# Cross-attention, layer 1: one set of token-wise exponentials, turned in 32x32 blocks by VectorE, in place of a second, key-wise set

## Chip, cores and metric

One core of one Trainium2 chip runs the kernel. The metric is the device time of one run in microseconds (us), as the median of several runs. Engines are named PE (TensorE, matrix multiplication; PEld is its weight loads), DVE (VectorE), ACT (ScalarE), POOL (GpSimd) and SP (SyncE, which issues most DMAs). All arithmetic is FP32.

## The reference, cut to what matters

Two cross-attention layers follow each other over the same 128 context rows per batch (B = 2, S = 2048 tokens, width 512).

```
def layer0(q, ctx, mask):              # 16 heads of 64
    qh, kh, vh = heads(q@Wq+bq), heads(ctx@Wk+bk), heads(ctx@Wv+bv)
    attn = einsum('bhqd,bhkd->bhqk', qh, kh) * mask
    attn = exp(attn - max(attn)) * mask
    attn = attn / (sum(attn, -1) + 1e-15)
    x = heads_joined(attn @ vh) @ Wo + bo + q
    return layernorm(x) * gamma + beta

def layer1(query, ctx):                # 16 heads of 32
    q, k, v = heads(query@Wq.T), heads(ctx@Wk.T), heads(ctx@Wv.T)
    logits = (1/sqrt(32)) * einsum('bhqd,bhkd->bhqk', q, k)
    attn = softmax(logits, -1)         # over 128 keys
    ctx1 = heads_joined(attn @ v)
    x = query + ctx1 @ Wo.T + bo
    return layernorm(x) * gamma + beta

out = layer1(layer0(x, ctx, mask), ctx)
```

## The kernel before

The 2 x 2048 tokens are cut into 8 blocks t of 512 tokens; a block has 4 sub-tiles i of 128 tokens. The 16 heads form 4 groups g of 4 heads r. The attention of layer 0 runs first, for all blocks, up to about 390 us. Then stages t = -1 to 7 follow. In stage t three blocks are worked on side by side: the softmax of layer 1 for block t, the output projection and the layer norm of layer 0 and then the queries of layer 1 for the blocks after it (n = t + 1, f = t + 2), and the output projection and layer norm of layer 1 for the block before it (l = t - 1).

The order is written by hand. `steps(t)` returns a list of steps, each a letter with its block and part, and `go` issues them one after the other; every engine executes its own instructions in the order in which they were issued, and waits where one needs a result of another engine. So a step's place in the list is its place in all queues at once, those of the DMAs on SP too.

The letters that matter here:

- X, `maxima(t, g)`: token-wise scores. 16 matmuls (L873) with 32 rows of weights (the queries of 128 tokens) and 128 columns (the keys) on four row tiles of the array put scores of 128 tokens x (4 heads, 4 sub-tiles, 128 keys) into the two PSUM tiles `sc0` and `sc1`. DVE takes the maximum over the keys for heads 2 and 3 (L879) and scales it (`less`, L886), ACT takes eight exponentials (L889); DVE does the maximum for heads 0 and 1 (L893) and subtracts it (L894), ACT takes one exponential of 1024 elements (L897). The result `e` has its tokens on the partitions.
- U, `sums1(t, g)`: DVE adds up each head's 128 exponentials (2048 elements a partition, L903). G, `shares1(t)`: the reciprocals of all sums (L911), into `tops`, beside the maxima.
- M, `turn_maxima(t)`: PE transposes `tops` (L916), DVE copies it out (L918), and SP's queue writes the rows to DRAM and reads them back spread over partitions: per group 1 MB of maxima (`p1`) and 256 KB of shares (`r1`).
- S, `scores1(t, g)`: the same scores a second time, with the keys on the partitions: four matmuls (L948) of 512 columns into `sc0` and `sc1`; DVE subtracts the spread maxima (L967). P1, `exponentials1`: one ACT exponential of 2048 elements (L972).
- V, `attend1(t, g)`: four matmuls (L996) with a head's values (128 keys x 32) as weights and its 512 token columns of exponentials as data, one for each column tile of the array. VD, `scale1`: DVE multiplies the result by the spread shares (L1009).
- E, `project1` (L1026), Y, `rest1` (adds the residual, L1033), I, `moments1`, O, `norm1`, W, `store` (the output DMA): projection and layer norm of block l.
- Pr (`project0`, L671), J, K0, Z, N, R, L: the output projection of layer 0 and its layer norm. T/TW and Q, or TS/PQ/AQ (L822 to L852), turn the result and make the queries.

The last stage, t = 7, has no projections of later blocks. There no maxima are spread: X only takes maxima, and S subtracts them by four more matmuls with a constant matrix `sel` (L955); ACT takes the exponentials from PSUM; the sums come from matmuls with `ones` (L987); and C, `divide1`, takes the reciprocals of 512 columns on DVE (L1015) and multiplies (L1016). After stage 7 come, for block 7, the first halves of four projections, then the second halves, each with its residual, moments and norm.

The two lines that tie the step's place to the queues, and the buffers that S, X and (after the change) V share:

```
    def sc_tiles(name, shape):
        return [p_sc.tile([P, *shape], F32, tag=f"sc{n}", name=f"{name}_{n}") for n in range(2)]
    ...
    for t in range(-1, NB):
        go(steps(t))
```

The pool `p_sc` has one buffer for each tag, so a new user of the score tiles waits until the one before has been read. The values of layer 1 for both batches, `v1`, are made before the stages (L582, copied by ACT in L586) and stay in SBUF.

Of the kernel before, what the change touches and what calls it, by code (L numbers as in the profile page):

```python
# [16 lines left out]
P = 128  # L17
# [7 lines left out]
def two_cross_attentions(  # L25
# [81 lines left out]
    sel = const.tile([P, NG, K], F32, tag="sel", name="sel")  # L107
    for g in range(NG):
        for r in range(4):
            rows = slice(32 * r, 32 * (r + 1))  # L110
            nc.vector.tensor_scalar(
                sel[rows, g, :], ident[rows, 32 * r + g : 32 * r + g + 1].to_broadcast([32, K]),
                -1.0, None, ALU.mult,
            )
# [5 lines left out]
    v1 = const.tile([P, B, D], F32, tag="v1", name="v1")  # L120
# [27 lines left out]
    rows_dram = [dram.tile([2 * NG, 4, TB], F32, tag=f"rows_{t}", name=f"rows_{t}") for t in range(NB)]  # L148
# [57 lines left out]
    with tc.tile_pool(name="w1", bufs=1) as w1, tc.tile_pool(name="a2", bufs=2) as a2, tc.tile_pool(  # L206
# [372 lines left out]
        def values1(b):  # L579
# [6 lines left out]
            nc.scalar.copy(v1[:, b, :], ps)  # L586
# [279 lines left out]
    def maxima(t, g):  # L866
# [10 lines left out]
        to = tops.rearrange("p i (r n) -> p r i n", n=32)[:, :, :, g : g + 1]  # L877
        to = to.rearrange("p r i o -> p r (i o)")
        nc.vector.tensor_reduce(to[:, 2:], ps[1], AX.X, ALU.max)  # L879
        if t == NB - 1:  # L880
            nc.vector.tensor_reduce(to[:, :2], ps[0], AX.X, ALU.max)
            return

        e = fours.tile([P, 4, NQ, K], F32, tag="p1", name=f"e_{t}_{g}")
        less = three.tile([P, 2, NQ], F32, tag="less", name=f"less_{t}_{g}")
        nc.vector.tensor_scalar_mul(less, to[:, 2:, :], -scaling)  # L886
        for r in range(2, 4):
            for i in range(NQ):
                nc.scalar.activation(  # L889
                    e[:, r, i, :], ps[1][:, r - 2, i, :], AF.Exp, bias=less[:, r - 2, i : i + 1],  # L890
                    scale=scaling,
                )
        nc.vector.tensor_reduce(to[:, :2], ps[0], AX.X, ALU.max)  # L893
        nc.vector.tensor_tensor(  # L894
            e[:, :2], ps[0], to[:, :2, :].unsqueeze(3).to_broadcast([P, 2, NQ, K]), ALU.subtract
        )
        nc.scalar.activation(e[:, :2], e[:, :2], AF.Exp, scale=scaling)  # L897
        open_x[t, g] = e

    def sums1(t, g):  # L900

        to = sums.rearrange("p i r n -> p r i n")[:, :, :, g : g + 1]
        nc.vector.tensor_reduce(  # L903
            to.rearrange("p r i o -> p r (i o)"), open_x.pop((t, g)), AX.X, ALU.add
        )

    tTs, probs1, open_x = {}, {}, {}

    def shares1(t):
        share = tops.rearrange("p i (r n) -> p i r n", n=32)[:, :, :, NG : 2 * NG]  # L910
        nc.vector.reciprocal(share, sums)  # L911

    def turn_maxima(t):
# [5 lines left out]
        tTs[t] = tT  # L919
        if t == NB - 1:  # L920
# [307 lines left out]
```

## Time and profile before

| what | value |
|---|---|
| median of 3 runs | 981.69 us (980.66 to 983.73) |
| span of the profiled execution, first to last instruction | 977.3 us |
| profiled execution's own time | not listed apart from its span; the span lies 4.4 us under the median |
| mean granted PE clock | 0.997 |
| busy: PE, DVE, ACT, POOL | 958.0, 731.8, 414.9, 483.3 us |
| steady stages, start to start of X(t,0) | 643.27, 713.14, 783.03, 852.90: 69.9 us each |
| X(7,0), start of the last stage | 916.10 us |

A line of a timeline gives the start and the length of a run of like instructions, the engine, the line of the code, the operation, out<-in with the shapes, how many there were, and in brackets how long the engine was idle before and on whom it waited. Matmuls are listed by passes: an FP32 matmul is two.

### The profile page before, as it was taken

The page shows a single profiled execution, that of the slowest core. Times are in us where ns is not written, and L with a number is a line of the kernel's source. Part 1 is how long each engine was busy: PE and PEld are TensorE (multiplying, and loading weights), DVE is VectorE, ACT ScalarE, POOL GpSimd, SP SyncE. Part 2 cuts the span into 40 slices and gives each one's busy share as a digit, 9 for nine tenths or more (in the row PEclk, how much of TensorE's full clock was granted, in tenths as well). Part 3 has the DMA queues.
Part 4 walks back from the last instruction along what each step waited for, and adds up shares of the span by engine and source line. Part 5 has one row for each costly group of instructions (what it writes and reads, how often), then busy time and mean ns, then how long its engine had stood idle before and what let it go on. Part 6 is the DMA issues. An engine that isn't in the chain of part 4 may idle for free.

```text
span 977.3 us, 12755 instructions
## 1 busy us (share of the span) xinstructions
PE 958.0 (98%) x4628; PEld 448.4 (46%) x4628; DVE 731.8 (75%) x1093; ACT 414.9 (42%) x637; POOL 483.3 (49%) x403
## 2 busy tenths in 40 slices
PE   8999999999999999999999999999999999999996
PEld 4444333333333334474544644645545545545442
DVE  2577777878878872249469869879789689698867
ACT  1145345545534644044534434434344444344351
POOL 1044454543453546685453934925835736546153
PEclk9999999999999999999999999999999999999998
DMA  9314265225223436534632542632723724403311
GB/s 337 126 49 141 55 175 155 56 57 182 60 79 86 120 104 201 181 128 157 243 128 87 188 160 87 238 110 89 263 82 119 251 90 155 167 1 151 111 44 43
DMA packets 51325, 128.46 MB, mean 131 GB/s; under 512 B 9440, under 2 KB 13280, under 8 KB 47680
## 3 DMA queue, kind: packets, MB, share of 16 engines
q1 hardware_dynamic: 49536, 125.03, 38.5%
q0 software_dynamic: 1152, 2.10, 0.9%
q8 instruction: 36, 0.59, 0.3%
q10 hardware_dynamic: 576, 0.53, 0.2%
q14 instruction: 25, 0.20, 0.1%
HBM read 101.46 MB, written 26.18 MB: 131 GB/s over the span
## 4 chain that ended last, share of the span: by engine, by line
PE 76%; DVE 4%; POOL 2%; issue 1%; ACT 0%; POOLq 0%; DVEq 0%; ACTq 0%
PE pso L671 22%; PE ps L347 12%; PE pso L1026 10%; PE psq L822 8%; PE psu L491 5%; PE st L396 4%; PE s L948 3%; PE mx L873 3%; PE u L996 3%; PE psq L860 1%; PE tr L727 1%; PE den L470 1%; PE den L484 1%; DVE sums L903 1%; PE psk L591 1%
## 5 line engine op out<-in xcount | busy, mean ns | idle before, releaser
L435 POOL TENSOR_TENSOR sm<-sm,mask 128x1024 f32<-128x1024 f32 x64 | 150.4, 2372 | 202.4 <-ACT sm L434 191.4
L671 PE MATMUL pso<-wo,uT 128*128 128x512 f32 x512 | 229.2, 599 | 0.2 <-POOL uT L182 0.2
L671 PEld LDWEIGHTS pso<-wo,uT 128*128 128x128 f32 x512 | 94.5, 190 | 117.2 <-issue 109.1
L658 POOL TENSOR_TENSOR rstd<-rstd,mhalf 128x1 f32<-128x1 f32 x64 | 35.2, 550 | 213.8 <-DVE shift L662 213.7
L434 ACT ACTIVATE sm<-sm,ncs 128x1024 f32<-128x1024 f32 x64 | 70.0, 1141 | 107.6 <-DVE ncs L431 107.5
L1026 PE MATMUL pso<-wq,ctx 128*128 128x512 f32 x256 | 115.5, 600 | 0.0
L889 ACT ACTIVATE e<-mx,less 128x128 f32<-128x128 f32 x224 | 60.9, 383 | 83.6 <-DVE less L886 83.6
L972 ACT ACTIVATE p<-p 128x2048 f32<-128x2048 f32 x28 | 53.5, 1911 | 97.2 <-DVE p L967 79.5
L409 DVE CUSTOM_DVE_ANT_1 sm<-st,mask 128x1024 f32<-128x1024 f32 x64 | 75.6, 1217 | 20.9 <-DMA mask<-in_maskT_dram 13.5
L967 DVE TENSOR_TENSOR p<-s,p 128x1024 f32<-128x1024 f32 x56 | 65.8, 1217 | 29.2 <-PE s L948 28.6
L347 PE MATMUL ps<-xt,wq 128*128 128x512 f32 x180 | 83.4, 599 | 0.0
L359 DVE TENSOR_TENSOR q<-ps,q 128x512 f32<-128x512 f32 x75 | 51.9, 692 | 39.5 <-PE ps L347 35.3
L182 POOL TENSOR_TENSOR uT<-uT,r 128x1024 f32<-128x1024 f32 x32 | 75.3, 2362 | 3.7 <-issue 1.7
L1026 PEld LDWEIGHTS pso<-wq,ctx 128*128 128x128 f32 x256 | 46.5, 190 | 57.4 <-issue 48.6
L462 DVE TENSOR_TENSOR fold<-fold,sm 64x2048 f32<-64x2048 f32 x22 | 64.5, 2930 | 2.6 <-ACT fold L456 1.9
L903 DVE TENSOR_REDUCE sums<-e 128x16 f32<-128x2048 f32 x28 | 63.8, 2278 | 1.1 <-ACT e L897 1.1
L396 PE MATMUL st<-q,k 64*128 64x512 f32 x256 | 63.6, 615 | 0.0
L491 PE MATMUL psu<-sm,v 128*32 128x512 f32 x512 | 62.1, 598 | 0.8 <-ACT dens L441 0.7
L347 PE MATMUL ps<-t,s 128*128 128x512 f32 x120 | 56.4, 592 | 0.0
L347 PEld LDWEIGHTS ps<-xt,wq 128*128 128x128 f32 x180 | 33.2, 190 | 46.5 <-issue 46.4
L686 ACT ACTIVATE z<-z,shift,rstd 128x512 f32<-128x512 f32 x32 | 26.0, 814 | 66.9 <-POOL shift L663 66.9
L688 POOL TENSOR_TENSOR y<-z,g 128x512 f32<-128x512 f32 x32 | 40.6, 1269 | 23.1 <-ACT z L686 23.1
(154 smaller groups left out, 1511.0 us busy)
## 6 DMA issues: line engine op xcount, KB each, us to landing
p<-rows SPq DMA_DIRECT2D x28, 1024.0 KB
u<-u SPq DMA_DIRECT2D x32, 512.0 KB
uT<-u SPq DMA_DIRECT2D x32, 512.0 KB
xt<-in_xT_dram SPq DMA_DIRECT2D x16, 512.0 KB
z<-in_x_dram SPq DMA_DIRECT2D x32, 256.0 KB
r<-r SPq DMA_DIRECT2D x32, 256.0 KB
out_dram<-y SPq DMA_DIRECT2D x32, 256.0 KB
r<-rows SPq DMA_DIRECT2D x28, 256.0 KB
```

The source lines that it names most:

```text
L182: nc.gpsimd.tensor_tensor(u, u, r.unsqueeze(1).to_broadcast([P, 2, TB]), ALU.mult)
L347: nc.tensor.matmul(ps, w[:, c, :], x[c] if isinstance(x, tuple) else x[:, c, :], start=(c == 0), stop=(c == 1),)
L396: nc.tensor.matmul(st[n][:, j, :], k0[rows, 2 * g + n, b * K : (b + 1) * K], q[rows, :], start=True, stop=True,)
L409: nc.vector.tensor_tensor_reduce(out=sm, in0=st[n], in1=masks[t].unsqueeze(1).to_broadcast([P, 2, TB]), scale=1.0, scalar=-3.4028234e38, o ...
L434: nc.scalar.activation(s, s, AF.Exp, bias=ncs[:, i + n : i + n + 1])
L435: nc.gpsimd.tensor_tensor(s, s, masks[t].unsqueeze(1).to_broadcast([P, 2, TB]), ALU.mult)
L491: nc.tensor.matmul(ps[32 * j : 32 * (j + 1), :], v0[:, b, d : d + 32], p[j], start=True, stop=True,)
L671: nc.tensor.matmul(ps, uTs[t, n // 2][:, n % 2, i * P : (i + 1) * P], wo0s[n // 2][:, n % 2, :], start=(n == 0), stop=(n == NE - 1),)
L822: nc.tensor.matmul(ps[:, m, :], w[:, c, m * P : (m + 1) * P], y[:, c, :], start=(c == 0), stop=(c == 1),)
L903: nc.vector.tensor_reduce(to.rearrange("p r i o -> p r (i o)"), open_x.pop((t, g)), AX.X, ALU.add)
L967: nc.vector.tensor_tensor(p1[:, at], ps[n], p1[:, at], ALU.subtract)
L1026: nc.tensor.matmul(ps, ctxs[t][g][:, i * P : (i + 1) * P], wo1s[:, g, :], start=(g == 0), stop=(g == NG - 1),)
```

## The change

After the change, X, for all eight blocks, keeps its maxima to itself (`top`), and ACT adds up the eight exponentials of heads 2 and 3 while it makes them (`accum_out`); U adds up only heads 0 and 1. Then DVE transposes `e` in place, in 32x32 blocks (`blocks1`). After that each block of 32 tokens and 32 keys has the keys on its 32 partitions. So V multiplies 32 x 32 blocks: for each quarter k of the keys, each 32-partition row tile a (32 tokens of every sub-tile) and each head r (a column tile) a matmul with 32x32 weights and 128 columns, 64 in all on 16 array tiles, summed over k in the score tiles. For this the values must have each quarter of the keys on each 32 partitions: `v1` goes through DRAM into `v1r`, four copies. `scale1` puts the columns back into order in two instructions. S, P1, C, `sel`, the matmuls with `ones` and the spreading of the maxima go; M turns the shares alone.

In the last stage U also takes the reciprocals of its group's 16 sums, and multiplies `e` by them, on POOL for groups 0 and 1 and on DVE for 2 and 3, ahead of the transposition, which for groups 0 and 1 is a step of its own, UT. V's result is there only copied, one half by DVE and one by ACT. The lists of steps change as shown; V(0,3) moves from the start of stage 1 to the end of stage 0. The scratch for DMA descriptors made by software is set to 2048 bytes.

```diff
-    sel = const.tile([P, NG, K], F32, tag="sel", name="sel")
...
-    v1 = const.tile([P, B, D], F32, tag="v1", name="v1")
...
+    v1_dram = dram.tile([B, K, D], F32, tag="v1", name="v1")
+    rows_dram = [dram.tile([NG, 4, TB], F32, tag=f"rows_{t}", name=f"rows_{t}") for t in range(NB)]
...
-            nc.scalar.copy(v1[:, b, :], ps)
+            v = eight.tile([P, D], F32, tag="z", name=f"v1_{b}")
+            nc.scalar.copy(v, ps)
+            nc.sync.dma_start(v1_dram[b], v)
...
+        top = three.tile([P, 2, 2, NQ], F32, tag="top", name=f"top1_{t}_{g}")
+        less = three.tile([P, 2, NQ], F32, tag="less", name=f"less_{t}_{g}")
         e = fours.tile([P, 4, NQ, K], F32, tag="p1", name=f"e_{t}_{g}")
+        nc.vector.tensor_reduce(top[:, 1], ps[1], AX.X, ALU.max)
+        nc.vector.tensor_scalar_mul(less, top[:, 1], -scaling)
         for r in range(2, 4):
             for i in range(NQ):
                 nc.scalar.activation(
                     e[:, r, i, :], ps[1][:, r - 2, i, :], AF.Exp, bias=less[:, r - 2, i : i + 1],
-                    scale=scaling,
-                )
+                    scale=scaling, accum_out=sums[:, i, r, g : g + 1],
+                )
+        nc.vector.tensor_reduce(top[:, 0], ps[0], AX.X, ALU.max)
         nc.vector.tensor_tensor(
+            e[:, :2], ps[0], top[:, 0].unsqueeze(3).to_broadcast([P, 2, NQ, K]), ALU.subtract
         )
         nc.scalar.activation(e[:, :2], e[:, :2], AF.Exp, scale=scaling)
+        probs1[t, g] = e
 
     def sums1(t, g):
 
+        e = probs1[t, g]
+        to = sums.rearrange("p i r n -> p r i n")[:, :2, :, g : g + 1]
+        nc.vector.tensor_reduce(to.rearrange("p r i o -> p r (i o)"), e[:, :2], AX.X, ALU.add)
+        if t == NB - 1:
+            share = three.tile([P, NQ, 4], F32, tag="share", name=f"share_{t}_{g}")
+            nc.vector.reciprocal(share, sums[:, :, :, g])
+            engine = nc.gpsimd if g < 2 else nc.vector
+            engine.tensor_tensor(
+                e, e, share.rearrange("p i r -> p r i").unsqueeze(3).to_broadcast([P, 4, NQ, K]),
+                ALU.mult,
+            )
+        if t < NB - 1 or g > 1:
+            blocks1(t, g)
+
+    def blocks1(t, g):
+        flat = probs1[t, g].rearrange("p r i k -> p (r i k)")
+        nc.vector.transpose(flat, flat)
...
+    def turn_shares(t):
...
         for r in range(4):
-            nc.sync.dma_start(rows_dram[t][:, r, :], tT[32 * r : 32 * r + 2 * NG, :])
+            nc.sync.dma_start(rows_dram[t][:, r, :], tT[32 * r : 32 * r + NG, :])
         for g in range(NG):
...
+            r = three.tile([P, TB], F32, tag="r1", bufs=4, name=f"r1_{t}_{g}")
+            nc.sync.dma_start(r, rows_dram[t][g].unsqueeze(1).to_broadcast([4, 32, TB]))
+            dens1[t, g] = r
...
     def attend1(t, g, apart=False):
...
+        ps = sc_tiles(f"u1_{t}_{g}", [2, TB])
+        for k in range(4):
+            for a in range(4):
+                of = slice(32 * a, 32 * (a + 1))
+                for r in range(4):
+                    h = 4 * g + r
+                    nc.tensor.matmul(
+                        ps[a // 2][32 * r : 32 * (r + 1), a % 2, :P].rearrange("p (i q) -> p i q", q=32),
+                        v1r[of, b, k, h * HD : (h + 1) * HD], e[of, r, :, k, :],
+                        start=(k == 0), stop=(k == 3),
+                    )
         open_u[t, g] = ps
...
+    def by_rows(x):
+        return x.rearrange("p (i a q) -> p a i q", a=4, q=32)
 
     def scale1(t, g):
-        nc.vector.tensor_tensor(ctxs[t][g], open_u.pop((t, g)), dens1.pop((t, g)), ALU.mult)
+        ps = open_u.pop((t, g))
+        for n in range(2):
+            of = slice(2 * n, 2 * n + 2)
+            to = by_rows(ctxs[t][g])[:, of]
+            u = ps[n][:, :, :P].rearrange("p a (i q) -> p a i q", q=32)
+            if t == NB - 1:
+                (nc.scalar.copy if n else nc.vector.tensor_copy)(to, u)
+            else:
+                nc.vector.tensor_tensor(to, u, by_rows(dens1[t, g])[:, of], ALU.mult)
...
     def steps(t):
         n, f, l = t + 1, t + 2, t - 1
         if n == NB:
             return [
...
+                (X, t, 0), (E, l, 0, 0), (V, l, 3), (I, l - 1, 3), (O, l - 1, 3), (X, t, 1), (W, l - 1, 3),
+                (E, l, 0, 1), (Y, l, 0), (I, l, 0), (U, t, 0), (X, t, 2), (E, l, 1), (Y, l, 1), (I, l, 1), (O, l, 0),
+                (U, t, 1), (X, t, 3), (E, l, 2), (Y, l, 2), (I, l, 2), (UT, t, 0), (V, t, 0), (O, l, 1), (W, l, 0),
+                (E, l, 3, 0), (UT, t, 1), (U, t, 2), (V, t, 1), (O, l, 2), (W, l, 1), (E, l, 3, 1), (Y, l, 3),
+                (V, t, 2), (U, t, 3), (I, l, 3), (W, l, 2), (O, l, 3), (V, t, 3), (W, l, 3),
             ]
...
         return start + [
             (N, f, 0), (E, l, 2), (O, l, 0), (M, t), (TW, n), (Y, l, 2), (I, l, 2), (N, f, 1), (E, l, 3),
             (TS, n, 0), (TS, n, 1), (Y, l, 3), (I, l, 3), (PQ, n, 1), (O, l, 1), (PQ, n, 2), (O, l, 2), (N, f, 2),
...
+            (PQ, n, 6), (PQ, n, 7), (V, t, 0, True), (AQ, n, 6), (AQ, n, 2), (AQ, n, 7), (VD, t, 0), (N, f, 3),
+            (O, l, 3), (R, f, 0), (W, l, 0), (PQ, n, 5), (PQ, n, 4), (AQ, n, 5), (V, t, 1), (AQ, n, 4), (W, l, 1),
+            (PQ, n, 3), (AQ, n, 3), (Pr, f, 0, 0), (V, t, 2), (W, l, 2), (Pr, f, 0, 1), (V, t, 3), (W, l, 3),
+            (R, f, 1),
         ]
...
+    v1r = one.tile([P, B, 4, D], F32, tag="v1r", name="v1r")
+    for a in range(4):
+        nc.sync.dma_start(v1r[32 * a : 32 * (a + 1)], v1_dram.rearrange("b (k p) d -> p b k d", p=32))
 
     sums0(1, three, "r1", 4)
...
+    nc = bacc.Bacc("TRN2", target_bir_lowering=False, num_devices=1, dynamic_dma_scratch_size=2048)
```

## The prediction

> **What bounds the kernel now.** The page comes first, for the engines' shares and the chain of work that ended last. Times are microseconds.
>
> ```profile
> PE 958.0 (98%) x4628; PEld 448.4 (46%) x4628; DVE 731.8 (75%) x1093; ACT 414.9 (42%) x637; POOL 483.3 (49%) x403
> PE 76%; DVE 4%; POOL 2%; issue 1%; ACT 0%; POOLq 0%; DVEq 0%; ACTq 0%
> ```
>
> TensorE (PE) sets the end: less work there is worth its own time, as long as nothing else becomes late. But 75% of VectorE (DVE) is a mean. The windows view of one steady stage, cut where the token-wise scores end and `turn_maxima` (M) begins (columns: start:end, length, then busy time of PE, weight loads, DVE, ACT and POOL, granted clock, DMA share, GB/s):
>
> ```profile
> 643.27:679.00 35.73, 35.73 (x204) 17.20 (x201) 34.10 (x44) 16.19 (x40) 14.94 (x18) 1.00 0.26 93
> 679.00:713.14 34.14, 34.14 (x166) 18.88 (x164) 25.30 (x48) 13.71 (x14) 25.28 (x23) 1.00 0.62 214
> ```
>
> PE is full in both halves, and DVE is full in the first: 34.10 of 35.73. The change takes its DVE work out of the second half and puts new DVE work into the first. The timeline of PE in the second half, with the blocks it loses (L948), the blocks it remakes (L996), and the 32x128 matmuls of X (L873):
>
> ```profile
> 706.45 1.14 PE L948 MATMUL s<-q,k 32*128 32x512 f32 x8
> 707.52 1.06 PE L996 MATMUL u<-p,v 128*32 128x512 f32 x8
> 708.52 3.70 PE L671 MATMUL pso<-wo,uT 128*128 128x512 f32 x8
> 712.15 1.06 PE L996 MATMUL u<-p,v 128*32 128x512 f32 x8
> 713.14 1.17 PE L873 MATMUL mx<-k,q 32*128 32x128 f32 x32
> 714.25 7.13 PE L671 MATMUL pso<-wo,uT 128*128 128x512 f32 x16
> 721.31 1.17 PE L873 MATMUL mx<-k,q 32*128 32x128 f32 x32
> ```
>
> From start to start, S takes 1.07, V 1.00, X 1.10 and the cycle of the first half 8.17 (713.14 to 721.31). The counts are of passes, two for one matmul. The DVE timeline of one such cycle:
>
> ```profile
> 722.58 1.23 DVE L879 TENSOR_REDUCE tops<-mx 128x8 f32<-128x1024 f32 x1 [0.29 <-PE mx L873]
> 723.84 0.65 DVE L886 TENSOR_SCALAR less<-tops 128x8 f32<-128x8 f32 x1
> 724.41 1.21 DVE L893 TENSOR_REDUCE tops<-mx 128x8 f32<-128x1024 f32 x1
> ...
> 728.59 2.28 DVE L903 TENSOR_REDUCE sums<-e 128x16 f32<-128x2048 f32 x1
> 730.78 1.22 DVE L879 TENSOR_REDUCE tops<-mx 128x8 f32<-128x1024 f32 x1
> ```
>
> Its cycle is 8.20 (722.58 to 730.78) against PE's 8.17, and only 0.29 of it was a wait for PE. Last, the end of the kernel (timelines of PE and DVE):
>
> ```profile
> 952.53 1.24 PE L996 MATMUL u<-p,v 128*32 128x512 f32 x8
> 953.70 14.12 PE L1026 MATMUL pso<-wq,ctx 128*128 128x512 f32 x32
> ```
>
> ```profile
> 957.35 3.35 DVE L1015 RECIPROCAL dens<-dens 128x512 f32<-128x512 f32 x1
> 962.71 0.69 DVE L1033 TENSOR_TENSOR y<-pso,y 128x512 f32<-128x512 f32 x1 [1.22 <-PE pso L1026]
> ```
>
> The last V ends 37.6 after X(7,0) started (916.10), the closing Y starts 46.6 after it, and 14.6 later all ends (977.3).
>
> **TensorE, a steady stage (t = 1 to 5).** Four S go: 4 x 1.07, and 0.2 where two re-entries into 128-row weights vanish: -4.5. V becomes 64 matmuls, 128 passes of 32x32 weights and 128 columns. The nearest row is X: 32 passes of 128 columns on four row tiles take 1.10, that is 8 rounds of about 0.112 and 0.2 of entry. In X's records the passes of a round, on different tiles, start 7 ns apart, and a round is as long as one pass: 512 columns take 0.43 (L671, 7.06 for 16), so 128 take 0.11. With 16 tiles, 128 passes are again 8 rounds, and 16 starts of 7 ns fit in 0.112: 1.1 for V, +0.1 each, +0.4 a stage. No row has 16 tiles at once. The other bound is that only four run together: 32 rounds of 0.112 and 0.2, 3.8, +2.8 for a V. I take 1.1, because a pace of one pass length per round of distinct tiles holds for one tile (L671), four row tiles (L873) and four column tiles (L996). PE: -4.1 a stage.
>
> [...]
>
> **VectorE, first half.** Per group the reduction of 2048 elements (L903, 2.19 to the next start) becomes one of 1024 (1.12, as L879), plus an in-place transposition of 128x2048. No row shows a transposition. Bounds: one 1024-element instruction (1.1) if two elements pass per cycle, twice the 2048-element reduction (4.4) if it needs two passes over the data. I take 2.2, the pace of every FP32 row here at that size. So +1.15 a group, +4.6 a stage. U(t,3) with its transposition stands before G, and G before M, so all four delay M. Cover: 0.29 of idle and about 0.4 between U(t,3) and M, 0.7. PE then waits 3.9 at M, and TW, TS and the products behind M wait with it. ACT's half of the sums is free: 8 exponentials took 2.18 (L889), and with an accumulator read (L785 with accumulation: 0.09 more a piece) 2.8, beside a cycle of 8.17.
>
> The second half loses 8 subtractions (L967, 9.7 of its 25.3 on DVE) and ACT's L972 (7.6). Both were off the chain: nothing is gained there. The 28 broadcasts of 1 MB go too; their queue appears nowhere in the chain, so nothing. The loads of v1r (2 MB) stand on SP's queue ahead of those of sums0(1), which were issued at 398.7 and first used by DVE at 427: 2 MB at the page's mean of 131 GB/s is 16, so 28 of slack hides them; without it they would cost up to 16 once.
>
> **A new wait.** V now writes the two score tiles, which X of the next stage needs at once (L996 to L873, above). Between them come two half-size scalings on DVE (about 0.4 each, L1009 being 0.69 whole): and two handovers of about 0.1: 1.0, of which 0.2 is the entry of X that the pause hides, +0.8 a stage. Behind X on PE stands the next project0, and X's reductions on DVE wait as long. Lower bound nothing, upper 1.5.
>
> Steady stage: -4.1 + 3.9 + 0.8 = +0.6; five make +3. Stage 6 has the same terms and its PE was at points already waiting on DVE: +0.8.
>
> **Stage 0.** Here S waited too: 4 x 1.07, and 1.5 where one S block took 2.58 to the next start, -5.8; a part of the V waits on ACT (0.86 and 0.41) goes, -0.5; V +0.4; three groups' lateness at M, +2.7. Together -3.2.
>
> **The last stage.** Before, it only reduced maxima and did the exponentials key-wise on ACT. After, DVE carries everything up to V(7,3). From X(7,0): four X of 3.8 (L879 to L894, 714.41 to 718.22), 15.2; VD(6,3) 0.9 and I 1.1; three Y with I of 1.78 (L1033 0.71, statistics 1.07), 5.3; a fourth Y, 0.7; four U of 1.3, 5.2; four transpositions of 2.2, 8.8; two multiplications by the shares (2 x 1.22 each) 4.8; three copies of V, 1.3. Sum 43.3. Add the 1.3 before the first reduction, 2 for V(6,3), which now stands between X(7,0) and X(7,1) on the same score tiles, and `less` waiting for POOL: before, L886 took 0.17 to 1.03, ending with the POOL instruction then running, and POOL now runs two multiplications of about 4.7 (L182's 2.36 for 1024, doubled), 1.8 for one such wait, 3.6 for two. V(7,3) can start at 48.4 to 50.2 and ends 1.2 later; then project1's 7.06 and 1.76 as before: Y at 58.6 to 60.4 in place of 46.6, +12 to +14. I take +13. The four reciprocals of 3.35 that go (L1015) lay mostly beside this chain. Bounds +5 (no POOL wait, transpositions at 1.1) and +22 (at 4.4).
>
> **Sum.** -3.2 + 3 + 0.8 + 13 = +13.6. The profiled span of 977.3 would be 990.9. The median of the three runs, 981.69, lies 4.4 above that span; carried over: 995.3.
>
> **Rivals.**
> Forecast: 984 to 1012, chance 0.54.
> R1, faster: the transposition takes about 1.1, not 2.2. Then DVE's first half is no busier than before, M is not late, and a steady stage is -4.1 + 0.8 = -3.3 (five: -16.5, stage 0: -5.9, stage 6: -3.3), the last stage +13 - 4.4 = +8.6: -17, about 965 to 972. It decides below about 1.7, where the lateness of four groups is halved. For: only the missing row. Against: every FP32 row on DVE is near 1.1 per 1024. Chance 0.15.
> R0, near nothing: a transposition near 1.8 (lateness 3.9 - 1.6) and a tail of +8: 979 to 984, 0.09.
> R2, PE is the loser: 16 tiles do not run together. At four together, +2.8 x 32 = +90, less what DVE's lateness covers in the first half (nothing, V lies in the second): about 1075. Chance 0.07. In between (15 ns a start, +1.0 x 32): 1012 to 1030, 0.10.
> R3, the transposition at 4.4: +2.2 x 28 = +62 and +9 at the end, about 1065. Chance 0.05.
>
> The range 965 to 1030 leaves out R2's far case and R3, 12 in 100, and the edges. About 0.3%, 2.9, is what a measurement of this kernel can tell from no change. Faster 0.17 (R1 and a part of R0), same 0.08, slower 0.75.
>
> **What would show it.** L996's successor as a block of 1.1 with 128 passes; a DVE transposition of 2.2; DVE busy without a gap in the first half of a stage, and PE waiting about 4 for DVE at the transposes of the shares; about 1 of PE idle between V(t,3) and X(t+1,0); V(7,3) starting near 49 after X(7,0). The forecast is wrong if M does not wait (R1), or if V takes 2 or more (R2).

## The result, and the profile after

The changed kernel takes 1042.85 us (1041.65 to 1043.78) against 982.71 for the one before in the same runs: a ratio of 1.0612, 95% interval 1.0594 to 1.063. The direction was forecast, the size was not: +60 in place of +13.6. The profiled execution has a span of 1041.5, 64.2 more than before. The page after, engines and chain of work:

```profile
PE 967.9 (93%) x8144; PEld 490.7 (47%) x8144; DVE 714.3 (69%) x1094; ACT 385.3 (37%) x889; POOL 490.6 (47%) x405
PE 42%; DVE 27%; issue 3%; DMA 3%; ACT 1%; POOL 1%; POOLq 0%; ACTq 0%; DVEq 0%; SPq 0%
```

PE was 76% of the chain and is 42%, DVE was 4% and is 27%, and DMA, which was nowhere, is 3%. PE is now idle for 74 us of the span. Stage by stage, by the starts of the X blocks in the two traces:

| stretch | before | after | difference | forecast |
|---|---|---|---|---|
| start to X(0,0) | 433.8 | 453.3 | +19.5 | 0 |
| stage 0 | 68.4 | 69.5 | +1.1 | -3.2 |
| stage 1 | 71.2 | 72.2 | +1.0 | +0.6 |
| stages 2 to 5, each | 69.9 | 73.3 | +3.4 | +0.6 |
| stage 6 | 63.2 | 67.5 | +4.3 | +0.8 |
| X(7,0) to the first closing Y | 46.6 | 71.05 | +24.4 | +13 |
| from there to the end | 14.6 | 14.8 | +0.2 | 0 |

Three things cost: something ahead of X(0,0) that the forecast had at nothing, about 3 us a stage, and the last stage. (The start to X(0,0) varies between runs: 448.4 to 454.1 over the twelve kernels here that leave the loads of v1r in their place.)

The windows view of a steady stage, cut at X(t,0) and at the transposes of the shares, before and after:

```profile
643.27:679.42 36.15, 36.15 (x204) 17.34 (x201) 34.52 (x45) 16.19 (x40) 15.36 (x18) 1.00 0.26 92
679.42:713.14 33.72, 33.72 (x165) 18.74 (x163) 24.88 (x47) 13.71 (x14) 24.86 (x23) 1.00 0.63 216
```

```profile
668.28:708.49 40.21, 37.57 (x201) 17.72 (x201) 38.05 (x48) 18.66 (x72) 15.58 (x18) 1.00 0.22 72
708.49:741.58 33.09, 32.71 (x613) 23.11 (x613) 17.44 (x45) 6.29 (x10) 24.59 (x22) 1.00 0.31 108
```

The first half grew by 4.1, with DVE at 38.05 of 40.21; the second shrank by only 0.6, though four S blocks had left it. PE's timeline shows both: waits for DVE around the projections in the first half, and V blocks that are not 1.1 long in the second.

```profile
699.15 3.70 PE L979 MATMUL pso<-wq,ctx 128*128 128x512 f32 x8 [0.42 <-DVE z L672]
704.53 3.70 PE L979 MATMUL pso<-wq,ctx 128*128 128x512 f32 x8 [1.68 <-DVE y L986]
708.49 0.66 PE L918 MATMUL trm<-ident,tops 128*128 128x128 f32 x4 [0.25 <-DVE tops L913]
...
739.29 1.90 PE L946 MATMUL u<-e,v1r 32*32 32x128 f32 x128
741.58 1.49 PE L867 MATMUL mx<-k,q 32*128 32x128 f32 x32 [0.38 <-DVE ctx L967]
```

A V block takes 1.83 from its start to the next block's (2.28 to 2.29 where X follows at once), where S and V together had taken 2.07. The change thus saves 0.24 of PE a group. In stage 0, one V block was also interrupted by a pause of 1.80 that the profile puts to "issue". The DVE timeline of a cycle, with the transposition that no row of before had shown:

```profile
748.64 1.21 DVE L893 TENSOR_REDUCE sums<-e 128x8 f32<-128x1024 f32 x1
749.89 2.31 DVE L907 STREAM_TRANSPOSE e<-e 128x2048 f32<-128x2048 f32 x1
752.13 1.18 DVE L874 TENSOR_REDUCE top<-mx 128x8 f32<-128x1024 f32 x1
```

2.24 to the next start: the 2.2 of the forecast. At the other end of the layer-0 part, PE and POOL just ahead of X(0,0):

```profile
424.91 5.45 PE L854 MATMUL psq<-yT,wq 128*128 128x256 f32 x24 [0.46 <-ACT yT L705]
440.81 3.78 PE L854 MATMUL psq<-yT,wq 128*128 128x256 f32 x8 [10.45 <-ACT q L858]
```

```profile
436.54 2.34 POOL L174 TENSOR_TENSOR uT<-uT,r 128x1024 f32<-128x1024 f32 x1 [8.07 <-issue]
438.83 0.55 POOL L652 TENSOR_TENSOR rstd<-rstd,mhalf 128x1 f32<-128x1 f32 x1
```

PE stands still for 10.45 because ACT's copy of the queries waits behind a layer-norm activation, which waits for the tiny rstd step on POOL, which stands in POOL's queue behind a multiplication of uT. The bracket names "issue", nothing that the profile shows; what that multiplication waited for is left to an experiment.

Last, the end of the last stage on PE:

```profile
1004.85 1.90 PE L946 MATMUL u<-e,v1r 32*32 32x128 f32 x128 [1.27 <-DVE ctx L965]
1013.32 2.81 PE L946 MATMUL u<-e,v1r 32*32 32x128 f32 x128 [6.57 <-DVE e L907]
1016.05 15.77 PE L979 MATMUL pso<-wq,ctx 128*128 128x512 f32 x32
```

V(7,3) starts 57.7 after X(7,0) (955.66), not 48.4 to 50.2, and V and the projections themselves are slower: 2.81 and 15.77, where the projections had been 14.12. Four rows of DVE in this stage show waits for PE:

```profile
963.51 0.94 DVE L967 TENSOR_TENSOR ctx<-u,r 128x256 f32<-128x256 f32 x2 [2.77 <-PE u L946]
966.63 1.23 DVE L874 TENSOR_REDUCE top<-mx 128x8 f32<-128x1024 f32 x1 [1.12 <-PE mx L867]
994.77 0.42 DVE L965 COPY ctx<-u 128x256 f32<-128x256 f32 x1 [2.75 <-PE u L946]
1006.65 0.43 DVE L965 COPY ctx<-u 128x256 f32<-128x256 f32 x1 [1.26 <-PE u L946]
```

### The profile page after: what moved, and what is told of

The parts are those of the page before. It is cut to its first block, busy times and chain, and to the rows that moved or that the text cites. A ratio compares the mean times of both kernels' runs of the same rounds, so it can differ in the third digit from the quotient of the medians.

```text
span 1041.5 us, 19942 instructions
## 1 busy us (share of the span) xinstructions
PE 967.9 (93%) x8144; PEld 490.7 (47%) x8144; DVE 714.3 (69%) x1094; ACT 385.3 (37%) x889; POOL 490.6 (47%) x405
## 4 chain that ended last, share of the span: by engine, by line
PE 42%; DVE 27%; issue 3%; DMA 3%; ACT 1%; POOL 1%; POOLq 0%; ACTq 0%; DVEq 0%; SPq 0%
PE pso L665 8%; PE psq L816 7%; PE ps L339 6%; PE u L946 6%; DVE e L907 5%; DVE sums L893 3%; DVE top L874 3%; DVE e L883 3%; PE pso L979 3%; DVE top L882 3%; PE psq L854 3%; PE psu L483 2%; DVE bn L647 2%; PE st L388 2%; DMA r<-r 2%
## 5 line engine op out<-in xcount | busy, mean ns | idle before, releaser
L665 PE MATMUL pso<-wo,uT 128*128 128x512 f32 x512 | 228.8, 598 | 0.6 <-POOL uT L174 0.6
L878 ACT ACTIVATE e<-mx,less 128x128 f32<-128x128 f32 x256 | 90.0, 377 | 231.4 <-DVE less L875 225.8
L665 PEld LDWEIGHTS pso<-wo,uT 128*128 128x128 f32 x512 | 94.7, 190 | 111.8 <-issue 105.4
L979 PE MATMUL pso<-wq,ctx 128*128 128x512 f32 x256 | 124.6, 631 | 12.6 <-DVE y L986 10.1
L979 PEld LDWEIGHTS pso<-wq,ctx 128*128 128x128 f32 x256 | 48.6, 200 | 74.8 <-issue 51.3
L946 PE MATMUL u<-e,v1r 32*32 32x128 f32 x4096 | 64.9, 290 | 18.5 <-DVE e L907 11.2
L967 DVE TENSOR_TENSOR ctx<-u,r 128x256 f32<-128x256 f32 x56 | 21.2, 419 | 86.6 <-PE u L946 80.3
L907 DVE STREAM_TRANSPOSE e<-e 128x2048 f32<-128x2048 f32 x32 | 73.9, 2310 | 1.0
L946 PEld LDWEIGHTS u<-e,v1r 32*32 32x32 f32 x4096 | 50.9, 105 | 41.9 <-issue 33.6
L878 ACT ACTIVATION_READ_ACCUMULATOR e<-mx,less 128x1 f32 x256 | 55.3, 216 | 0.0
```

The source lines that it names most:

```text
L665: nc.tensor.matmul(ps, uTs[t, n // 2][:, n % 2, i * P : (i + 1) * P], wo0s[n // 2][:, n % 2, :], start=(n == 0), stop=(n == NE - 1),)
L878: nc.scalar.activation(e[:, r, i, :], ps[1][:, r - 2, i, :], AF.Exp, bias=less[:, r - 2, i : i + 1], scale=scaling, accum_out=sums[:, i, r ...
L907: nc.vector.transpose(flat, flat)
L946: nc.tensor.matmul(ps[a // 2][32 * r : 32 * (r + 1), a % 2, :P].rearrange("p (i q) -> p i q", q=32), v1r[of, b, k, h * HD : (h + 1) * HD], ...
L979: nc.tensor.matmul(ps, ctxs[t][g][:, i * P : (i + 1) * P], wo1s[:, g, :], start=(g == 0), stop=(g == NG - 1),)
```

## Experiments

Each is an edit of the changed kernel unless said otherwise. Kernels with one run are read by their traces.

**1. The loads of v1r, later (a1).**

```diff
-    for a in range(4):
-        nc.sync.dma_start(v1r[32 * a : 32 * (a + 1)], v1_dram.rearrange(...))
...
+                (J, n, 2), (Pr, n, 3, 0), (Pr, n, 3, 1), (J, n, 3), *fetches, (spread_values, t), (U, t, 3), (G, t),
```

> The changed kernel with the four loads of v1r issued in stage 0 (after the fetches of u) instead of ahead of sums0(1). After the change the first X(0,0) started at 453.3 us against 433.8 before: +19.5, which the prediction had costed at nothing. Theory: the 2 MB of v1r loads stand on SP's queue ahead of the loads that layer 0's last normalisations need, so r, z and uT land late, the POOL multiplication by r is late, and the tiny rstd step behind it in POOL's queue holds up the layer norm of block 0. Then X(0,0) returns to 433 to 436 and the whole run is 17 to 20 shorter than the changed kernel (about 1024). Rival: the delay comes from v1's way through DRAM itself (the ACT copies and stores of v1, on SP ahead of the last u); then X(0,0) stays at 445 or later and the run at 1035 or more.

X(0,0) starts at 436.36, the span is 1022.6 (18.9 less), the median of two runs 1027.09 (15.8 less), a ratio of 1.0453 (1.0386 to 1.0521) to the kernel before. PE's wait for ACT's copy is down to 1.31:

```profile
426.07 1.99 PE L854 MATMUL psq<-yT,wq 128*128 128x256 f32 x8 [1.31 <-ACT q L858]
```

The rival's store and copies of v1 stayed in place, so the theory holds: it was the four loads, about 17 of the 19.5. All traces agree: the twelve kernels with the loads in place start X(0,0) at 448.4 to 454.1, the four with the loads moved (a1, c1, c2, c3) at 433.9 to 436.8. Against a1, 5.6 of the 17 were lost ahead of the first queries (424.91 against 419.31), 9.1 in the stretch with the long wait, and 2.2 after it: the clock granted to PE was 0.50 from 441 to 445, with PE full.

**2. What a V block consists of (a2, a3, a5, a6, a7, a8).** Six kernels change V alone. First, each matmul cut into two of 64 columns:

```diff
-                        ps[a // 2][32 * r : 32 * (r + 1), a % 2, :P]..., e[of, r, :, k, :],
+                        ps[a // 2][32 * r : 32 * (r + 1), a % 2, 64 * c : 64 * c + 64]..., e[of, r, 2 * c : 2 * c + 2, k, :],
```

> The changed kernel with every V matmul cut into two of 64 columns: 256 passes in place of 128, the same columns in all. Measured after the change: a V block takes 1.83 us from start to next, not 1.1; its first 32 passes start 6.7 ns apart, the rest about 13.6 ns a pass. Theory A: V is bound by the rate at which PE is fed with pairs of weight load and matmul (13.6 ns a pass); then a V block takes 3.4 to 3.8, +1.7 each, and the run is some +55 longer than the changed kernel. Theory B: V is bound by the columns that stream through the array (128 a pass), tiles overlapping less than 16-fold; then a V block stays at 1.8 to 2.2 and the run within 10 of the changed kernel.

The three V blocks that were unbroken and not followed by an X took 2.65 for 256 passes, start to next: less than theory A's doubling, more than theory B's no growth. One more was unbroken, ahead of an X. The other 28 of 32 were torn apart by 33 pauses, most of them 1.7 to 3.5 and 70.9 together, that the profile puts to "issue". The run took 1194.83, 152 more than the changed kernel; the pauses and the longer V (32 times 0.82, 26) make up 97 of that, and the mean clock granted was 0.92 in place of 0.976. One of the torn blocks:

```profile
624.12 2.60 PE L947 MATMUL u<-e,v1r 32*32 32x64 f32 x243
628.46 0.34 PE L947 MATMUL u<-e,v1r 32*32 32x64 f32 x13 [1.75 <-issue]
```

All these pauses fall at one place of PE's program. Counted in PE's records (weight loads, matmuls and waits for semaphores), each comes after the 193rd or 194th of a run of 256, and so do both pauses in V blocks of the changed kernel (1.80 and 0.72). The instruction queue of the pages (q8) moved 96 packets here and 64 in the changed kernel, for 24,618 and 16,426 such records, that is about 256 records a packet. That the pauses belong to the passage from one such packet to the next is the author's inference from these counts; no run tests it, or why only some passages would cost time.

Next, the order of the tiles alone, rows in the inner loop:

```diff
-            for a in range(4):
-                for r in range(4):
+            for r in range(4):
+                for a in range(4):
```

> The changed kernel with V's two inner loops exchanged: consecutive matmuls go to different row tiles of one column tile, not to different column tiles of one row tile. Theory A (a rate of pairs of weight load and matmul): a V block stays at 1.83 within 0.05 and the run within 3 us of the changed kernel. Theory B (neighbours in the same row tile wait for each other): a V block falls to 1.1 to 1.4, -0.4 to -0.7 each, -13 to -22 in all; or it rises if neighbours in one column tile are the ones that wait.

V stayed at 1.83 and the run at 1039.47; neighbours in one row tile wait no more for each other than neighbours in one column tile.

Then eight tiles in turn in place of 16:

```diff
-        for k in range(4):
-            for a in range(4):
+        for k, a in [(k, a) for two_rows in ((0, 1), (2, 3)) for k in range(4) for a in two_rows]:
```

> The changed kernel with V's loops reordered so that row tiles 0 and 1 do all four quarters of the keys before row tiles 2 and 3: the same 128 passes of 128 columns, but eight tiles take turns, not 16. Measured so far for 16 passes: 0.217 us with 128 columns, 0.155 with 64, in the same order of tiles. Theory A: a 32x32 tile cannot load its next weights (records of 0.10) while it streams (0.107), so a round lasts load plus stream, 0.21, however many tiles take part; then 16 rounds make a V block 3.3 to 3.7, and the run is 40 to 55 longer than the changed kernel. Theory B: passes are fed at 13.6 ns each, whatever tile they go to; then a V block stays at 1.83 within 0.1 and the run within 4.

V took 1.96, a little above theory B's band of 1.83 and 0.1; a round of load plus stream in each tile (A) falls. Twice the columns, and four tiles in turn:

```diff
-                        e[of, r, :, k, :],
+                        e[of, r, :, k, :].unsqueeze(1).to_broadcast([32, 2, NQ, 32]),
```

> The changed kernel with every V matmul streaming its 128 columns twice (256 columns a pass; the second half goes to an unused half of the PSUM bank). Passes, tiles and order stay. Measured so far per pass: 13.6 ns with 128 columns, whether 16 or 8 tiles take turns; 9.7 with 64. Theory A: passes are fed at about 13.6 ns, and 16 tiles do run at once (a pass of 256 columns lasts 0.213; 0.213 / 16 = 13.3); then a V block stays at 1.8 to 2.1. Theory B: only eight passes are in the array at a time (0.107 / 8 = 13.4; with 64 columns another floor, 9.7); then 26.7 a pass, a V block of 3.5 to 3.8. Theory C: feed and stream add up (5.8 + 0.061 ns a column, the line through the two measured points); then 21.4 a pass, 2.8 to 3.1.

V took 2.69: theory C's sum of a fixed part and the columns, though a little under its band; not a rate of feeding, and not eight at a time.

```diff
-        for k in range(4):
-            for a in range(4):
+        for a in range(4):
+            for k in range(4):
```

> The changed kernel with V's loop over the row tiles outermost: only the four column tiles of one row tile take turns. Theory B (as many passes at once as there are distinct tiles, up to eight): 0.107 / 4 = 26.8 a pass, a V block of 3.5 to 3.8, +45 to +55 in all. Theory A (a rate of feeding alone, whatever the tile, with passes to one tile queued behind each other without loss) needs at least 26.8 here too, since four tiles cannot stream faster; so a block that stays below 3 would fell both.

V took 2.69 again, below the 3 that would fell both theories. The records hint at why: rounds of four go on about 0.11 apart for eight rounds, the last of which starts at 0.79, but a second set of four passes starts 0.49 after the block's start, between them. The records do not name the array tile; if these are the next row tile's, its passes start while the first has three rounds of its own still to go. That gave a new theory, which fitted all five after the fact: about 16 passes are under way at once, each from the start of its weight load (records of 0.105) to the end of its stream (0.107 for 128 columns, an estimate: a quarter of the 0.43 from start to start of L665's 512-column passes), and a tile streams one pass at a time. With both edits, eight tiles and 256 columns, it says something else than a fixed part plus columns:

> The changed kernel with both edits to V: eight tiles take turns (row tiles 0 and 1, then 2 and 3), and every pass streams 256 columns. V blocks measured so far, start to next: 16 tiles 2.65 (256 passes of 64 columns), 1.83 (128 of 128), 2.69 (128 of 256); eight tiles of 128 columns 1.96; four tiles of 128 columns 2.69. Theory W (about 16 passes are under way at a time, each from the start of its weight load, a record of 0.105, to the end of its stream of 0.107 for 128 columns; and a tile streams one pass at a time): 0.212 / 16 = 13.3 ns a pass for 128 columns, 9.9 for 64, 19.9 for 256, and eight tiles of 256 columns are bound by the tile, 0.213 / 8 = 26.7 ns: a V block of 3.4 to 3.8. Rival C (6.4 ns plus 0.052 ns a column for each pass, whatever the tiles): 19.7 ns, a V block of 2.6 to 2.8.

V took 3.45, in the band of theory W and far from the rival's 2.6 to 2.8. This fits a tile that streams one pass at a time (0.213 / 8 is 26.6 ns a pass, measured 3.45 / 128, 27.0) and says nothing of the number 16. And the start of a block does not fit W as it stands: in the changed kernel the first 32 passes start within 0.233, while the record of each lasts 0.27 to 0.29, so by the records 32 are under way there. W describes the times of whole blocks; what sets them is not shown. The V records of a6, and below of a8 (their lengths include the end of the last pass):

```profile
729.05 2.76 PE L946 MATMUL u<-e,v1r 32*32 32x256 f32 x128
```

```profile
664.72 3.52 PE L946 MATMUL u<-e,v1r 32*32 32x256 f32 x128
```

Same passes, same columns; only how many tiles take turns differs.

**3. Transpositions in the second half (a4).** U no longer transposes in stages 0 to 6; UT steps stand ahead of each V.

```diff
-        if t < NB - 1 or g > 1:
+        if t == NB - 1 and g > 1:
             blocks1(t, g)
...
+            (TS, n, 0), (TS, n, 1), (Y, l, 3), (I, l, 3), (UT, t, 0), (PQ, n, 1), ...
```

> The changed kernel with the transpositions of stages 0 to 6 taken out of U and put into the second half of the stage, each some steps ahead of its V. Measured after the change: the first half of a steady stage (X(t,0) to the transposes of the shares) takes 40.2 against 35.7, PE waiting there on DVE. Theory: the four transpositions of 2.31 make DVE late for M, as the prediction had it (3.9 of lateness); then the first half returns to 36 to 37.5 (the pause between V(t,3) and X stays, about 0.8), the second half stays within 0.5 of 33.1, and the run is 17 to 25 shorter than the changed kernel. Rival: the waits come from ACT, whose eight exponentials now also read an accumulator, and X's score tiles come free late; then the first half stays above 39 and the run within 6.

The first half fell from 40.2 to 36.3 (by this cut it was 36.15 before the change), the second stayed at 33.0:

```profile
660.92:697.24 36.32, 36.32 (x200) 17.70 (x201) 31.39 (x52) 18.80 (x73) 16.45 (x21) 1.00 0.21 72
697.24:730.28 33.04, 32.66 (x614) 23.04 (x612) 23.70 (x40) 6.01 (x10) 23.61 (x20) 1.00 0.33 115
```

PE is full in the first half again with ACT's accumulator reads still there, so the rival falls. A stage takes 69.36 (one of the four steady ones 69.84), 0.5 less than before the change. The median of two runs is 1020.74, a ratio of 1.0389 (1.0317 to 1.0461).

**4. The last stage (b1 to b4).** Copies of V(7,g) on ACT alone:

```diff
-                (nc.scalar.copy if n else nc.vector.tensor_copy)(to, u)
+                nc.scalar.copy(to, u)
```

> The changed kernel, but in the last stage ACT copies both halves of V's result. Measured after the change: from X(7,0) to the first closing Y 71.05 us against 46.6; DVE waits for PE ahead of its copies of V(7,0) (2.75) and V(7,2) (1.26), waits that the prediction did not price. Theory: these waits are in the chain, since the transpositions and multiplications stand behind the copies in DVE's queue; then X(7,0) to Y is 67 to 69, and the run 3 to 4 shorter than the changed kernel. Rival: PE, at a lower granted clock, is what the chain runs through, and DVE merely waits elsewhere; then less than 1.

X(7,0) to Y: 69.87, only 1.2 less and in neither theory's band, though V(7,3) started at 53.97, 3.7 earlier. The clock was at 0.67 to 0.82 in the 10 us windows of this stage, and V(7,3) had a pause of 1.0 (after the 193rd of 256 records).

Matmuls added where PE waits (result never read):

```diff
+    def keep_busy(_, n):
+        idle = av_tile("idle")
+        for _ in range(n):
+            nc.tensor.matmul(idle, ident, wo1s[:, 0, :], start=True, stop=True)
...
+                (X, t, 0), (E, l, 0, 0), (KB, t, 2), (V, l, 3), (I, l - 1, 3), ...
```

> The changed kernel with 21 matmuls of 128x128 by 512 added in the last stage (2, 2, 3, 6, 1 and 7 of them, where PE waits 2.1, 1.7, 2.4, 4.7, 1.3 and 6.6 us for DVE); their result is never read. Measured after the change: the granted clock of PE falls to 0.67 to 0.84 after X(7,0), where it was 1.00 before the change, and V blocks take up to 3.1 and the closing projections 10.7 from V(7,3) to Y in place of 8.9. Theory: the clock falls because PE idles in the last stage, and costs 4 to 7 there; then with the waits filled the clock is 0.95 or more until the last projections, and X(7,0) to Y is 64 to 68 in place of 71.05. Rival: the lower clock hits only work that waits for DVE anyway; then X(7,0) to Y is 70 or more.

X(7,0) to Y: 67.47, 3.6 less, by doing more. The clock came back only in part (0.83 to 1.00 over the stage), but was 1.00 in the closing projections, and Y came 10.7 after V(7,3)'s start in place of 13.4. The added matmuls also cost something themselves: the last seven ended 1.4 after the transposition that V(7,3) needs (1010.10 and 2.31 of DVE), where V(7,3) had followed it by 0.15 in the changed kernel. So, by estimate, 3.6 is less than what the lower clock cost.

```profile
1005.93 7.97 PE L1088 MATMUL idle<-wq,ident 128*128 128x512 f32 x14
1013.83 1.91 PE L946 MATMUL u<-e,v1r 32*32 32x128 f32 x128
```

Both edits together:

> The changed kernel with both edits of the last stage: the 21 added matmuls (their result is never read) and both halves of V's copies on ACT. X(7,0) to the first closing Y took 71.05 after the change, 69.87 with the copies on ACT alone, 67.47 with the matmuls alone. With the copies on ACT, V(7,3) started 53.97 after X(7,0) in place of 57.66, but from there to Y it took 15.9 in place of 13.4, at a granted clock of 0.7 to 0.8 and with a pause of 1.0 inside V. Theory: clock and waits on copies are separate costs of about 3.6 each, and the lower clock only hid the second; then V(7,3) starts at 53 to 54.5, Y comes 10.5 to 11 later, X(7,0) to Y is 63.5 to 65.5. Rival: with the copies gone from DVE, PE waits more in places that the added matmuls do not fill, the clock falls again, and X(7,0) to Y stays above 66.5.

63.26, V(7,3) at 52.5: 7.8 less than the changed kernel, more than the two alone (4.8), and 0.2 below the theory's band. So the lower clock had hidden the gain of the copies. Here too the last seven added matmuls held V(7,3) up, by 1.3. The windows of the end, of the changed kernel and of this one (columns as above; the clock is the third number from the right):

```profile
1005.00:1015.00 10.00, 3.44 (x222) 2.91 (x216) 7.77 (x10) 0.37 (x1) 1.22 (x3) 0.72 0.08 28
1015.00:1025.00 10.00, 10.00 (x78) 4.60 (x50) 0.42 (x1) 1.19 (x2) 2.58 (x3) 0.77 0.08 28
```

```profile
1005.00:1018.66 13.66, 13.66 (x157) 6.61 (x156) 2.48 (x5) 1.46 (x3) 3.27 (x4) 1.00 0.06 20
```

In the changed kernel the clock was 0.72 in the 10 us in which PE was busy for 3.44, and 0.77 in the 10 us after, with PE full; with both edits it was 1.00 from 1005.00 to 1018.66, with PE full. These are means: in two other windows of the changed kernel the granted clock is 0.50 and 1.00. PE stood still from 1006.75 to 1013.32, and the clock was 0.50 from 1009.5 to 1019.6:

```profile
1009.50:1019.60 10.10, 6.29 (x132) 3.65 (x133) 5.03 (x7) 1.19 (x2) 3.27 (x4) 0.50 0.02 7
1019.70:1029.90 10.20, 10.20 (x25) 4.50 (x24) 3.06 (x7) 0.44 (x1) 0.74 (x2) 1.00 0.04 16
```

Then the same without the multiplications by the shares:

```diff
-            engine = nc.gpsimd if g < 2 else nc.vector
-            engine.tensor_tensor(e, e, share..., ALU.mult)
```

> The same, and the multiplications of block 7's exponentials by their shares are left out (block 7's attention is not normalised). Two of them run on DVE (3.30 and 2.29 after the change), two on POOL, and the scaling less behind POOL's took 2.69, 0.68 and 0.89 in place of about 0.15. Theory: all of this is in the chain of the last stage: 5.6 and 3.5 to 3.8 less, so X(7,0) to Y is 8 to 10 shorter than the run with both edits. Rival: only DVE's own two are, 5 to 6.

X(7,0) to Y: 60.35, 2.9 less than b3: neither theory. The added matmuls had become the bound: V(7,3) started at 1007.24, directly behind the last seven of them, while its transposition had ended 4.5 earlier. On DVE the last transposition ends 45.1 after X(7,0) in place of 51.1, so the multiplications and `less` cost DVE 6.0; what that is worth to the end was not measured.

**5. Together (c1 to c3).** These keep the change for blocks 0 to 6 and take the last stage as it was before; transpositions as in a4, loads of v1r late, V(6,3) at the end of stage 6.

> The changed kernel with the loads of v1r late, the transpositions in the second half of the stages, V(6,3) at the end of stage 6, and the last stage as it was before the change (key-wise scores for block 7 with sel, sums by ones, divisions), beside the new one for blocks 0 to 6. If the three costs named so far (v1r loads +17, lateness in the first halves +21, last stage +24) add up and nothing else is hidden, X(7,0) starts at 917 to 920, X(7,0) to Y is 46 to 48, and the run is 980 to 986, that is, the time of the kernel before within 0.4%. If the last stage is slow for another reason than its DVE work, X(7,0) to Y stays above 52.

982.2, a ratio of 1.0017 (1.0003 to 1.003) to the kernel before. X(7,0) at 920.43, to Y 45.95, both within 0.5 of the forecast: the costs add up, except that stage 0 took 72.9, because V(0,0) now waited for v1r and V(0,1) for the shares that were loaded behind it. So the loads went to an earlier place, after which the DMA engines had been less busy in c1 (a share of 0.26 from 445 to 455 and 0.02 from 455 to 460):

```diff
-... *fetches, (spread_values, t), (U, t, 3), (G, t),
+                (X, t, 1), (J, n, 0), (K0, n, 0), *loads, (spread_values, t), (WS, n, 0), ...
```

> The last combination (late transpositions, the old last stage) with the v1r loads issued after stage 0's loads of residuals and shares, where the DMA engines are idle for about 10 us, instead of after the fetches of u. There, V(0,0) waited 1.6 for v1r and V(0,1) 2.6 for a scaling held up by the r loads behind v1r; stage 0 took 72.9 against 66.7 in the run with only the late transpositions. Theory: those waits go; stage 0 takes 66 to 68, the run is 975 to 978, that is 0.4 to 0.7% faster than the kernel before. Rival: the loads of r, z and u run into v1r again; then stage 0 stays at 70 or more and the run at 980 or more.

Stage 0 took 67.4 as expected, but the run did not show it: 982.01, ratio 1.0011 (0.9986 to 1.0035), its span 979.8. X(0,0) came 2.3 later in this profile than in c1's, and stages 1 and 6 took 0.6 and 2.0 more. Last, V(t,2) and V(t,3) one projection half earlier, and the transpositions of groups 2 and 3 earlier too:

```diff
-            (PQ, n, 3), (AQ, n, 3), (UT, t, 3), (Pr, f, 0, 0), (V, t, 2), (W, l, 2), (Pr, f, 0, 1), (V, t, 3), ...
+            (PQ, n, 3), (AQ, n, 3), (V, t, 2), (Pr, f, 0, 0), (W, l, 2), (V, t, 3), (Pr, f, 0, 1), ...
```

> The same, and in stages 1 to 5 V(t,2) and V(t,3) stand each one projection half earlier, so that 3.6 us of other matmuls lie between V(t,3) and X(t+1,0), which share the score tiles; the transpositions of groups 2 and 3 stand earlier too. Measured so far: X(t,0) waits 0.4 for the scaling and takes 0.3 longer than the other X, V(t,3) to X 2.28 in place of 1.83. Theory: 0.7 to 0.9 a stage is gained, five stages 3.5 to 4.5. Rival: the earlier V wait for their transposition on DVE, and the stage stays at 69.4 or grows.

977.59, a ratio of 0.9955 (0.9941 to 0.997): about 4.7 less than the kernel before, clear of noise but under 0.5%. A steady stage takes 68.81, 0.6 less than c2's (0.7 to 0.9 had been expected) and 1.07 less than before the change, and X follows without a wait:

```profile
706.90 1.91 PE L1009 MATMUL u<-e,v1r 32*32 32x128 f32 x128
712.37 1.17 PE L878 MATMUL mx<-k,q 32*128 32x128 f32 x32
```

## Why the prediction was wrong, point by point

- **Lateness of DVE in the first half: right in size, not in place.** The first half was to grow by 3.9 and grew by 4.1; moving the transpositions away gave back 3.9 of it (a4). But PE did not wait about 4 at M: it waited 0.23 ahead of X(t,3), 0.42 and 1.68 ahead of two projections, whose buffers DVE's residual additions free, and 0.25 at M. The transposition was taken at 2.2 and is 2.24. The reason given, that every FP32 row of DVE is near 1.1 per 1024 elements, does not hold for all (the reciprocal of 512, L1015, takes 3.35), so some luck is in that value.
- **The price of V: wrong, and the largest error of the steady stage.** The step "8 rounds of 0.112" took the pace of X for one of 16 tiles. X's rounds of four tiles start 0.112 apart, near the 0.107 of one stream (a quarter of the 0.43 of 512 columns); with 16 tiles something else sets the pace (the six times of V fit some 16 pairs of load and stream under way, a limit that was inferred and not seen), and a V is 1.83, not 1.1. Four times 0.73 is 2.9, and a steady stage missed by 2.8: the second half was to shrink by 3.3 and shrank by 0.6. Stage 0 missed by 4.3, of which the same 2.9 and a pause of 1.80 are the largest parts. The price lies between the bounds given (1.1 and 3.8), and the rival that came nearest, "15 ns a start", had been given 0.10.
- **"16 starts of 7 ns": right for the first passes alone.** The first 32 passes of a V start mostly 6.7 ns apart, within 0.233 in all, but 128 passes take 1.83, 14.3 ns each. The 7 ns are the distance of the passes within one round of X, whose mean pace is 34 ns (32 passes in 1.10); the row had been read too far.
- **V to X: right in kind**: 0.4 of wait and an X block 0.3 longer, 0.7 for the forecast 0.8; c3, which puts other matmuls between, gained 0.6.
- **"28 of slack hides the loads of v1r": wrong, +17.** The step looked at the consumer of the next DMA in the queue (sums on DVE at 427) and not at all that stand behind: r, z and uT. uT is multiplied on POOL, and behind that in POOL's queue stood block 0's rstd, and behind that PE. The upper bound named there (16, the time of 2 MB) was nearly the price, but not carried into the range; that it came so near is in part luck, since 2.2 of the 17 are the lower clock after the wait.
- **The last stage: +13 forecast, +24.4 measured, outside the bounds of +5 to +22.** DVE's work was summed as if it ran without gaps. V(7,3) started some 8 later than forecast, and from there to Y it took 13.4 in place of 10.2. DVE waited for PE ahead of VD(6,3) (2.77), X(7,1) (1.12), and the copies of V(7,0) (2.75) and V(7,2) (1.26): 7.9, of which 2 had been priced. The `less` steps took 0.68, 2.69 and 0.89, near the upper of the two cases; one multiplication on DVE took 3.30, the other 2.29; POOL's two took 3.64 each. And nothing had priced the clock: PE, idle more often, ran at 0.67 to 0.84 in the mean of 10 us, which cost at least 3.6 (b2), and 6.6 with the copies on ACT (b3 against b1).
- **No rival had the loads of v1r, the waits on DVE or the clock.** R1 fell with the transposition at 2.31; R2's far case and R3 did not happen, though R3's sum was near the measured time for another reason. Two sums are slightly off, without weight here: R2's far case comes to 995.3 + 90 = 1085, not 1075, and Y in the last stage to 58.4 to 60.2 from the terms named.

## What to carry to other kernels

Loads put into a queue can delay what stands behind them (here X(0,0) by about 17, the changed kernel against a1), so follow each later transfer to its consumer, and in the consumer's queue to what stands behind that. A sum of busy times on an engine is only a lower bound where its work alternates with another engine's (here V(7,3) was forecast at 48.4 to 50.2 after X(7,0) and started at 57.7); each handover needs its own line. A pace measured at one shape need not hold at another (here 8 rounds of 0.112 and 0.2, read from four tiles, became 1.83 on 16): ask what the next limit is, and put the chance there.

## What the runs showed of the hardware

- Small passes on the 16 tiles of PE: 1.83 for 128 passes of 128 columns (the changed kernel), 2.69 with 256 columns (a6), 1.96 with eight tiles (a5), 2.69 with four (a7), 3.45 with eight tiles and 256 columns (a8), and 2.65 for 256 passes of 64 columns (a2). These block times agree with some 16 passes under way between weight load and end of stream, but the number was inferred from them, and at the start of a block 32 passes start within 0.233.
- In the last stage of the changed kernel the mean clock granted to PE was 0.67 to 0.84 in windows of 10 us of which PE was busy for 34 to 83%, and 0.77 from 1015 to 1025, with PE full; in other windows it was 0.50 from 1009.5 to 1019.6 and 1.00 from 1019.7 to 1029.9. With added matmuls whose result is never read it was 0.83 to 1.00, and the stage 3.6 shorter (b2).
- 28 of 32 V streams of 256 small passes were interrupted by pauses, most of 1.7 to 3.5 us, that the profile puts to "issue" (a2); the changed kernel has two in its V blocks, 1.80 and 0.72. All come after the 193rd or 194th of a run of 256 PE records, and the instruction queue (q8) moved about one packet for each 256 of them (96 packets in a2, 64 in the changed kernel, 36 before); that the two belong together was not tested.
- DVE's scalar step `less`, 0.17 long where POOL did not multiply (b4, the same step of X(7,2)), took 2.69 beside POOL's 128x2048 multiplication and ended with it (974.30 and 3.64 of POOL against 975.27 and 2.69 of DVE).
